# Layer 1 FFN: the down projection as seven products per half of the tokens, in program order

## The chip, the cores and the metric

The kernel runs on one core of one Trainium2 chip. The metric is the device time of one execution in microseconds (us). The core has five engines with queues of their own: PE (TensorE, matmuls), DVE (VectorE), ACT (ScalarE), POOL (GpSimd) and SP, which here issues DMAs. Only PE writes to PSUM by matmul; DVE and ACT read PSUM and SBUF; POOL works on SBUF.

## What is computed

Two layers over 2 x 1024 tokens of 512 dimensions, all in f32. Only the last part of layer 1 is touched:

```python
def _L1_ffn_ref(x, w_gate, w_up, w_down):
    h = jax.nn.silu(jnp.einsum('bsh,hi->bsi', x, w_gate)) * jnp.einsum('bsh,hi->bsi', x, w_up)
    h_sparse = _sparsify_2to4(h)   # of each four neighbours in i, the two largest by |h| stay
    return jnp.einsum('bsi,ih->bsh', h_sparse, w_down)

x = x + _L1_attn_ref(xn, ...) + _L1_ffn_ref(xn, ...)
```

`w_gate` and `w_up` are 512 x 2048, `w_down` is 2048 x 512.

## The kernel before

**Tiles.** The 2048 tokens are four blocks of 512, taken in two pairs (`pb`). The 2048 hidden dimensions are `G` = 4 groups of 512, so that there are eight groups of work in order (0 to 7: pair 0, then pair 1). A group has two units (`half` 0 and 1, "even" and "odd" units below; units 0 to 15), each of which computes 256 hidden dimensions for a pair of blocks. The order of the hidden dimensions is chosen so that the four members of a sparsity group lie in four chunks of the same partition: `h[:, c, :]`, c = 0..3.

**Gate and up.** `gate_up` computes a unit by Strassen's algorithm in the form of Winograd: seven products instead of eight. Each product is 4 matmuls of 128x128 weights and 512 columns. `combine_w` makes the four sums of weights (`s`) on POOL, `combine_x` the sums of tokens (`t_c`) on DVE. Three pairs of PSUM banks (`pa`, `pb`, `pc`) hold the products. On PE the order in a unit is: product 1 (`w1` x, to `pa`), 2 (`s[0]` `tt[0]`, to `pc`), 3 (`s[1]` `tt[1]`, to `pa`), 4 (`w1` x, to `pb`), 5 (`s[2]` `tt[2]`, to `pa`), 6 (`w2` `tt[3]`, to `pa`), 7 (`s[3]` y, to `pc`). ACT copies `pa` to SBUF after products 1 (L206), 3 (L214) and 5 (L219); DVE adds `pb` to the first copy (L201), `pc` to the third (L220) and to the second (L230). Silu is on ACT (L194), the multiplication by the up half on DVE (L197). After product n the helper calls `hook(n - 1)` (after the fourth, its add comes first): what `hook` issues stands there in the order.

**Sparsify.** Twelve steps over [128, 4, 512] of one block and group: one ACT operation (`ab`, absolute values, L1187) and eleven on DVE: `hi`, `lo` (L1188, L1189), two compares `first` (L1191, L1192), two into `both` (L1194, L1195), `way` (L1196), two adds to `first` (L1197, L1198), and two that set the smaller members of `h` to zero (L1201).

**Down.** `down` makes 128 tokens of one block: four matmuls of 512 columns (the chunks of a group) into one of two PSUM banks, then one DVE add to the residual `x1` (L1211), and in a pair's last group the store. Eight such calls belong to a group. `hook` issues up to four sparsify steps at a time and one or three downs at hooks 4 and 6 of a later unit.

**Order.** In this stage the framework's scheduler orders each engine's instructions; the layer 0 FFN and the attention use `in_program_order`, which chains the instructions of each of PE, DVE, ACT and POOL as the program issues them. The attention's last output projections (L828) all use the same PSUM bank, with a DVE add (L1017) after each; passes of unit 0 stand between them on PE.

**Transfers.** SP loads gate/up weights (`gu`, two tiles of 512 KB per unit, four buffers in the stage's own pool), down weights (`wd`, 1 MB per group, two buffers), and issues the stores, each as soon as what it waits for is done, in its queue's order.

Of the kernel before, what the change touches and what calls it, by code (L numbers as in the profile page):

```python
# [9 lines left out]
F32 = mybir.dt.float32  # L10
BF16 = mybir.dt.bfloat16
AF = mybir.ActivationFunctionType
ALU = mybir.AluOpType
PSUM = bass.MemoryType.PSUM

P = 128
B, S, D = 2, 1024, 512
N = B * S
TT = 512
# [4 lines left out]
G = 4  # L24
# [11 lines left out]
def two_layers(ctx: ExitStack, tc: tile.TileContext, t: dict, out: bass.AP):  # L36
# [8 lines left out]
    def mark():  # L45
        return len(nc.cur_bb.bb.instructions)
# [28 lines left out]
    def ps_bank(name, which):  # L75

        return ps.tile([P, 512], F32, tag=f"bank{which}", name=name)
# [68 lines left out]
    def combine_x(pool, x, y, name):  # L146

        tt = [
            pool.tile([P, 2, TT], F32, tag=f"t{n}", name=f"t{n}_{name}") for n in (1, 2, 4)
        ]  # L150
        tt.insert(2, y[:, :2, :])

        def first():
            nc.vector.tensor_sub(tt[0], y[:, :2, :], x[:, :2, :])  # L154
            nc.vector.tensor_sub(tt[1], y[:, 2:, :], tt[0])

        def second():
            nc.vector.tensor_sub(tt[2], y[:, 2:, :], y[:, :2, :])
            nc.vector.tensor_sub(tt[3], x[:, 2:, :], tt[1])

        return tt, first, second

    def combine_w(pool, w1, w2, name):
        s = [
            pool.tile([P, 2, 2, P], F32, tag=f"s{m}", name=f"s{m}_{name}") for m in range(1, 5)
        ]
        nc.gpsimd.tensor_add(s[0], w2[:, :, :2, :], w2[:, :, 2:, :])  # L167
        nc.gpsimd.tensor_sub(s[1], s[0], w1[:, :, :2, :])
        nc.gpsimd.tensor_sub(s[2], w1[:, :, :2, :], w2[:, :, :2, :])
        nc.gpsimd.tensor_sub(s[3], w1[:, :, 2:, :], s[1])  # L170
        return s
# [79 lines left out]
    with tc.tile_pool(name="a", bufs=1) as a:  # L251
# [355 lines left out]
        def down(n, i, half):  # L607


            h, js = h0[n, i], (2 * half, 2 * half + 1)  # L610
            up = i in hf_t and (i, half) not in joined
            if up:
                joined.add((i, half))
            banks = two_banks(f"acc_{n}_{i}_{half}")
            for bank, j in zip(banks, js):
                for m in range(2):
                    nc.tensor.matmul(  # L617
                        bank, h[:, m, j * P : (j + 1) * P], w2h[:, :, 2 * (n % NU) + m, :],
                        start=(m == 0), stop=(m == 1 and not up),
                    )  # L620
            if up:
                for bank, j in zip(banks, js):
                    rows = slice(32 * j, 32 * j + R + 1)
                    nc.tensor.matmul(
                        bank, hf_t[i][rows, j * P : (j + 1) * P], wup_aug[rows, :],
                        start=False, stop=True,
                    )
            for bank, j in zip(banks, js):
                r = x1[i][:, j, :]
                nc.vector.tensor_add(r, r, bank)  # L630
# [3 lines left out]
        def some_downs(n):  # L634
            for _ in range(min(n, len(downs))):
                down(*downs.pop(0))
# [514 lines left out]
                f(*args)  # L1151


    with tc.tile_pool(name="c", bufs=1, reuse_waits="tile") as c_:
        units = [(pb, g, half) for pb in range(2) for g in range(G) for half in range(2)]
        gu_w = dict(first_gu)

        def load_gu(n, m):

            pb, g, half = units[n]  # L1160
            w = gu_w[n, m] = c_.tile([P, 2, KC, P], F32, tag="w", name=f"gu_{n}_{m}", bufs=4)
            nc.sync.dma_start(out=w, in_=t["gu"][4 * g + 2 * half + m])

        wd = {}

        def load_down(n):

            g = n % G
            wd[n] = c_.tile([P, 4, D], F32, tag="wd", name=f"wd_{n}", bufs=2)
            nc.sync.dma_start(  # L1170
                out=wd[n],
                in_=t["down"][g * GW : (g + 1) * GW, :].rearrange("(p r) d -> p r d", r=4),
            )

        def sparsify(h, name):

            ab = c_.tile([P, 4, TT], F32, tag="ab", name=f"ab_{name}")
            pair = ab.rearrange("p (q two) n -> p q two n", two=2)
            hi = c_.tile([P, 2, TT], F32, tag="hi", name=f"hi_{name}")
            lo = c_.tile([P, 2, TT], F32, tag="lo", name=f"lo_{name}")  # L1180
            first = c_.tile([P, 4, TT], BF16, tag="first", name=f"first_{name}")
            win = first.rearrange("p (q two) n -> p q two n", two=2)
            both = c_.tile([P, 2, TT], BF16, tag="both", name=f"both_{name}")
            way = c_.tile([P, TT], BF16, tag="way", name=f"way_{name}")
            wide = way.unsqueeze(1).to_broadcast([P, 2, TT])
            v = nc.vector
            yield nc.scalar.activation(ab, h, AF.Abs)  # L1187
            yield v.tensor_tensor(hi, pair[:, :, 0], pair[:, :, 1], ALU.max)  # L1188
            yield v.tensor_tensor(lo, pair[:, :, 0], pair[:, :, 1], ALU.min)  # L1189

            yield v.tensor_tensor(win[:, :, 0], pair[:, :, 0], pair[:, :, 1], ALU.is_ge)  # L1191
            yield v.tensor_tensor(win[:, :, 1], pair[:, :, 0], pair[:, :, 1], ALU.is_lt)  # L1192

            yield v.tensor_tensor(both[:, 0], lo[:, 0], hi[:, 1], ALU.is_ge)  # L1194
            yield v.tensor_tensor(both[:, 1], lo[:, 1], hi[:, 0], ALU.is_gt)  # L1195
            yield v.tensor_sub(way, both[:, 0], both[:, 1])  # L1196
            yield v.tensor_add(first[:, 0:2], first[:, 0:2], wide)  # L1197
            yield v.tensor_sub(first[:, 2:4], first[:, 2:4], wide)  # L1198
            for q in range(2):
                c = slice(2 * q, 2 * q + 2)  # L1200
                yield v.scalar_tensor_tensor(h[:, c], first[:, c], 1.0, h[:, c], ALU.is_ge, ALU.mult)  # L1201

        def down(h, w, i, j, store):

            po = ps_bank(f"po_{w.name}_{i}_{j}", j % 2)
            for r in range(4):
                nc.tensor.matmul(  # L1207
                    po, h[:, r, j * P : (j + 1) * P], w[:, r, :], start=(r == 0), stop=(r == 3)
                )
            x = x1[i][:, j, :]  # L1210
            nc.vector.tensor_add(x, x, po)  # L1211
            if store:
                row = i * TT + j * P
                nc.sync.dma_start(out=out[row : row + P, :], in_=x)

        tt = None
        steps, downs = [], []

        def some_steps(n):

            while n and steps:
                if next(steps[0], None) is None:
                    steps.pop(0)
                else:
                    n -= 1

        def some_downs(n):
            for _ in range(min(n, len(downs))):
                down(*downs.pop(0))

        for n, (pb, g, half) in enumerate(units):
            i0, i1 = 2 * pb, 2 * pb + 1
            x, y = xt1[i0], xt1[i1]
            if g == half == 0:
                tt, *make = combine_x(c_, x, y, f"c{pb}")
                for f in make:
                    f()
            if n == 0:
                for m in range(2, 6):
                    load_gu(m // 2, m % 2)  # L1240
                load_down(0)
            if half == 0:
                h = [
                    c_.tile([P, 4, TT], F32, tag="h", name=f"h_{n}_{m}", bufs=4) for m in range(2)
                ]

            def hook(at):
                if at < 3 or half == 0 and at > 4:
                    some_steps(4)
                if at in (4, 6):  # L1250
                    some_downs(1 if at == 4 else 3)

            w1, w2 = gu_w.pop((n, 0)), gu_w.pop((n, 1))
            gate_up(
                c_, f"c{n}", w1, w2, combine_w(c_, w1, w2, f"c{n}"), x, y, tt,
                lambda m, i: h[i][:, 2 * half + m, :], hook,
            )
            if 1 <= n and n + 2 < len(units):
                load_gu(n + 2, 0)
                load_gu(n + 2, 1)  # L1260
            if half == 0 and n + 2 < len(units):
                load_down(n // 2 + 1)
            if half == 1:
                for m, i in enumerate((i0, i1)):
                    steps.append(sparsify(h[m], f"{n}_{m}"))
                    downs += [(h[m], wd[n // 2], i, j, g == G - 1) for j in range(NJ)]
        some_steps(12)
        some_downs(4)
        some_steps(12)
        some_downs(4)  # L1270


# [69 lines left out]
```

## Time and profile before

| | |
|---|---|
| median of 3 runs | 1920.13 us (1920.07 to 1932.04) |
| the profiled execution | 1923.83 us, its span 1922.1 us |
| mean granted TensorE clock | 0.987 |
| layer 1 FFN, first to last of its matmuls | about 1285 to 1918 us |
| DVE busy in an even and an odd unit (1404.0 to 1441.8, 1441.8 to 1479.5) | 24.5 and 14.6 us |
| POOL busy in the same two | 6.8 and 6.0 us |

The page gives, from one profiled execution, the busy time of each engine, its costliest groups of instructions (line, engine, tiles, shape, count, busy time, mean of one, and the idle time of the engine before them with what ended it), and the chain of work that ended last. A timeline row is: start in us, duration in us, engine, line, operation, tiles, shape, how many were merged, and in brackets the idle time before it and what ended it. A line number is one of the listing; where a helper issues the instruction, it is the helper's.

### The profile page before, as it was taken

To read this page: it belongs to the slowest core of one execution; us is meant where nothing else is said; L and a number is where in the kernel's file an instruction comes from. 1 tells how busy PE (TensorE), PEld (TensorE's weight loads), DVE (VectorE), ACT (ScalarE), POOL (GpSimd) and SP (SyncE) were. 2 spreads that over 40 slices of the span, in tenths; PEclk is the share of its full clock that TensorE was granted. 3 is DMA by queue.
4 is the path that set the end of the run, shared out by engine and by line. 5 is a ranking of instruction groups with operands and counts; after the bars stand their busy time and mean duration, and the time that the engine had idled before them with its cause. 6 is when DMAs were issued, how large, how long until landed. Compare 5 with 4: busy or idle time off the path is not lost.

```text
span 1922.1 us, 17085 instructions
## 1 busy us (share of the span) xinstructions
PE 1852.8 (96%) x6652; PEld 789.8 (41%) x6652; DVE 987.9 (51%) x1346; ACT 462.6 (24%) x646; POOL 610.8 (32%) x568
## 2 busy tenths in 40 slices
PE   6999999999999998999999989999999999999998
PEld 4444444444444443333333333334444444444443
DVE  3574353343443334755666656663753654735625
ACT  3221121111221111244333333331221211211210
POOL 3222232213432101366676647731111112111200
PEclk9899999999999999999999989999999999999999
DMA  6121111000100100000000000020111101211101
GB/s 231 39 77 33 33 33 33 22 22 33 43 29 23 43 5 23 1 12 12 1 12 12 24 11 12 12 77 0 44 44 33 55 26 62 77 33 44 44 1 44
DMA packets 29456, 68.00 MB, mean 35 GB/s; under 512 B 3392, under 2 KB 11584, under 8 KB 27840
## 3 DMA queue, kind: packets, MB, share of 16 engines
q1 hardware_dynamic: 28656, 66.61, 10.5%
q8 instruction: 53, 0.87, 0.2%
q10 hardware_dynamic: 720, 0.30, 0.1%
q14 instruction: 27, 0.22, 0.0%
HBM read 62.70 MB, written 4.19 MB: 35 GB/s over the span
## 4 chain that ended last, share of the span: by engine, by line
PE 87%; DVE 7%; issue 2%; ACT 2%; POOL 1%; DMA 1%; ACTq 0%; DVEq 0%; POOLq 0%
PE p_a L177 19%; PE p_c L177 18%; PE acc L617 12%; PE po_wd L1207 10%; PE pq L828 6%; PE m L880 4%; PE s L933 4%; PE o L975 3%; PE po L828 3%; PE pv L828 2%; DVE tops L888 1%; PE w L995 1%; POOL acc L983 1%; PE s L939 1%; DVE m L887 1%
## 5 line engine op out<-in xcount | busy, mean ns | idle before, releaser
L617 PE MATMUL acc<-w2h,h 128*128 128x512 f32 x512 | 230.1, 594 | 3.9 <-DVE y L529 1.8
L983 POOL TENSOR_TENSOR acc<-acc,pt 128x1024 f32<-128x1024 f32 (+3 forms) x138 | 233.7, 1715 | 0.0
L1207 PE MATMUL po_wd<-wd,h 128*128 128x512 f32 x512 | 226.5, 596 | 3.5 <-DVE h L1201 2.9
L888 DVE TENSOR_REDUCE tops<-m 128x2 f32<-128x1024 f32 (+2 forms) x192 | 180.8, 955 | 59.4 <-PE m L880 54.9
L630 DVE TENSOR_TENSOR x<-x,acc 128x512 f32<-128x512 f32 x128 | 86.2, 685 | 177.0 <-PE acc L617 140.3
L950 ACT ACTIVATE pt<-s 128x1024 f32<-128x1024 f32 (+3 forms) x160 | 115.0, 766 | 179.9 <-PE s L939 175.1
L1207 PEld LDWEIGHTS po_wd<-wd,h 128*128 128x128 f32 x512 | 97.7, 191 | 127.8 <-issue 119.0
L617 PEld LDWEIGHTS acc<-w2h,h 128*128 128x128 f32 x512 | 96.5, 190 | 124.1 <-issue 115.8
L828 PE MATMUL pq<-xt,wqk 128*128 128x512 f32 x256 | 128.1, 627 | 4.7 <-ACT qk L844 3.9
L887 DVE TENSOR_TENSOR m<-m,mask 128x256 f32<-128x256 f32 x128 | 54.7, 427 | 135.5 <-PE m L880 110.9
L177 PE MATMUL p_a<-t_a,s_a 128*128 128x512 f32 x256 | 119.6, 612 | 2.7 <-DVE t_a L154 2.7
L177 PE MATMUL p_a<-xt,w 128*128 128x512 f32 x256 | 119.7, 611 | 0.7 <-ACT xt L134 0.7
L177 PE MATMUL p_c<-xt,gu 128*128 128x512 f32 x256 | 116.2, 592 | 0.0
L177 PE MATMUL p_a<-xt,s_a 128*128 128x512 f32 x256 | 115.3, 593 | 0.0
L177 PE MATMUL p_c<-xt,s_c 128*128 128x512 f32 x256 | 115.1, 592 | 0.0
L177 PE MATMUL p_c<-t_c,s_c 128*128 128x512 f32 x256 | 112.5, 592 | 1.1 <-DVE t_c L154 1.1
L933 PE MATMUL s<-qk,qk 32*128 32x512 f32 (+3 forms) x768 | 99.8, 538 | 13.1 <-DVE tops L888 13.1
L880 PE MATMUL m<-qk,qk 32*128 32x512 f32 (+3 forms) x768 | 102.8, 536 | 5.9 <-ACT acc L950 3.0
L167 POOL TENSOR_TENSOR s_c<-gu 128x512 f32<-128x512 f32 x16 | 32.2, 2010 | 215.7 <-PE p_c L177 215.7
L177 PEld LDWEIGHTS p_a<-t_a,s_a 128*128 128x128 f32 x256 | 49.7, 197 | 66.5 <-issue 65.0
L177 PEld LDWEIGHTS p_a<-xt,w 128*128 128x128 f32 x256 | 49.1, 196 | 64.1 <-issue 63.1
L828 PEld LDWEIGHTS pq<-xt,wqk 128*128 128x128 f32 x256 | 44.8, 193 | 73.7 <-issue 61.2
(206 smaller groups left out, 2353.9 us busy)
## 6 DMA issues: line engine op xcount, KB each, us to landing
w<-in_W SPq DMA_DIRECT2D x32, 512.0 KB, 3.7
gu<-in_gu SPq DMA_DIRECT2D x32, 512.0 KB, 3.6
wd<-in_down SPq DMA_DIRECT2D x8, 1024.0 KB, 5.0
x<-in_x SPq DMA_DIRECT2D x16, 256.0 KB, 4.2
w2h<-in_W2q SPq DMA_DIRECT2D x4, 1024.0 KB, 11.8
xr<-in_x SPq DMA_DIRECT2D x16, 256.0 KB, 2.7
wqk<-in_WqkvT SPq DMA_DIRECT2D x16, 256.0 KB, 3.2
out_x<-x SPq DMA_DIRECT2D x16, 256.0 KB, 2.0
```

Source lines behind the costliest of these rows:

```text
L177: nc.tensor.matmul(pair[:, m, :], a[:, m, k, :], x[:, k, :], start=start and k == 0, stop=stop and k == 1, skip_group_check=True,)
L617: nc.tensor.matmul(bank, h[:, m, j * P : (j + 1) * P], w2h[:, :, 2 * (n % NU) + m, :], start=(m == 0), stop=(m == 1 and not up),)
L630: nc.vector.tensor_add(r, r, bank)
L828: nc.tensor.matmul(got[0], lhs(k), rhs(k), start=(k == 0), stop=(k == KC - 1))
L880: nc.tensor.matmul(pair[h // 2][:, h % 2, :e], q[rows, qt * P : (qt + 1) * P], k[rows, c * 512 : c * 512 + e], start=True, stop=True,)
L887: nc.vector.tensor_add(d, d, mask.unsqueeze(1).to_broadcast([P, 2, P]))
L888: nc.vector.tensor_reduce(out=tops[u][:, c, qt, 2 * p : 2 * p + 2], in_=pair[p][:, :, :e], axis=mybir.AxisListType.X, op=ALU.max,)
L933: nc.tensor.matmul(pair[h // 2][:, h % 2, s:], k[rows, kt * P : (kt + 1) * P], q[rows, cols], start=True, stop=False,)
L950: nc.scalar.activation(pt[:, :, s:], pair[p][:, :, s:], AF.Exp, scale=1.0 / math.sqrt(HD))
L975: nc.tensor.matmul(po[rows, s:], v[:, rows], pts[h // 2][:, h % 2, s:], start=(kt == 0), stop=last, tile_position=(0, h * HD),)
L983: eng.tensor_add(acc[:, :, s:], acc[:, :, s:], pt[:, :, s:])
L1207: nc.tensor.matmul(po, h[:, r, j * P : (j + 1) * P], w[:, r, :], start=(r == 0), stop=(r == 3))
```

## The change

The down projection of groups 0 to 6 becomes seven products as well. A half of the tokens of each block (`half`, 256 tokens of both blocks) is one problem: the 2 x 2 quarters of `h` are (block 0 or 1) x (chunks 0, 2 or 1, 3), the quarters of `wd` are (those chunks) x (halves of the 512 dimensions). `down_weights` makes four sums of weights per group on POOL (one in place), `down_hidden` four sums of hidden values per half on DVE (one in place). A product m (0 to 6) is four matmuls of 256 columns. Products alternate over the two banks: 0 and 2 accumulate in bank 0, 1 in bank 1, 3 and 5 in bank 1, 4 and 6 in bank 0. After product 0 ACT copies the bank; after product 1 DVE adds the copy and the bank to `u2`; after each of 2 to 6 DVE adds the bank to a quarter of the residual; POOL adds `u2` to three quarters (`add_u2`). Group 7 stays with plain matmuls (`row_down`).

`h` is one tile for both blocks, and sparsify goes by halves of tokens instead of by blocks. All is issued at places written out by hand: place p of group n is hook p mod 7 of unit 2n + 2 + p div 7. The second half's last products so fall into the next even unit (hooks 0, 1, 2 and 4), the first half's products 0 and 1 at hooks 5 and 6 of the even unit. What is left of group 6 stands behind unit 15, a sparsify step of group 7 between any two products, and then group 7. The stage is put in program order. `combine_w` of the next unit is issued at hook 5, `combine_x` of the second pair at unit 7's hook 5 and unit 8's start. Gate/up weights alternate between two buffers of the stage's pool and the two `wqk` buffers, and are loaded when the unit two before is done.

```diff
+    start2 = mark()
     with tc.tile_pool(name="c", bufs=1, reuse_waits="tile") as c_:
...
+        def load_gu(n):
+            pb, g, half = units[n]
+            for m in range(2):
+                pool, tag = (c_, "w") if n % 2 else (res, "wqk")
+                w = gu_w[n, m] = pool.tile([P, 2, KC, P], F32, tag=tag, name=f"gu_{n}_{m}", bufs=2)
+                nc.sync.dma_start(out=w, in_=t["gu"][4 * g + 2 * half + m])
...
+        def down_weights(n, last):
+            w11, w12, w21, w22 = quarters_w(n)
+            if not last:
...
+                nc.gpsimd.tensor_sub(td[n][0], w12, w11)
+                nc.gpsimd.tensor_sub(td[n][1], w22, td[n][0])
+                nc.gpsimd.tensor_sub(w12, w22, w12)
+            else:
+                nc.gpsimd.tensor_sub(td[n][2], w21, td[n][1])
+
+        def down_hidden(n, half):
...
+            nc.vector.tensor_sub(s3, h11, h21)
+            nc.vector.tensor_add(h21, h21, h22)
+            nc.vector.tensor_sub(s2, h21, h11)
+            nc.vector.tensor_sub(s4, h12, s2)
...
+        def down(n, half, m):
...
+            lhs, rhs = (
+                (h11, w11), (s2, t2), (h12, w21), (s1, t1), (s3, t3), (s4, w22), (h22, t4)
+            )[m]
...
+            for j in range(2):
+                for q in range(2):
+                    nc.tensor.matmul(
+                        out_[:, j, :], lhs[:, q, j * P : (j + 1) * P], rhs[:, q, :],
+                        start=m in (0, 1, 3, 4) and j == q == 0, stop=j == q == 1,
+                        skip_group_check=True,
+                    )
+            at = {2: (0, 0), 3: (1, 1), 4: (1, 1), 5: (0, 1), 6: (1, 0)}.get(m)
+            if m == 0:
...
+                nc.scalar.copy(held_d["e1"], out_)
+            elif m == 1:
...
+                nc.vector.tensor_add(held_d["u2"], held_d["e1"], out_)
+            else:
+                r = residual(n, half, *at)
+                nc.vector.tensor_add(r, r, out_)
+
+        def add_u2(n, half, *quarters):
+            for q in quarters:
+                r = residual(n, half, *q)
+                nc.gpsimd.tensor_add(r, r, held_d["u2"])
...
+        for n in range(groups - 1):
+            end = n == groups - 2
+            for half, steps in enumerate((
+                ((0, 1), (1, 4), (2, 4), (3, 3)), ((5, 1), (6, 3), (7, 3), (8, 3), (9, 2))
+            )):
+                for at, count in steps:
+                    put1(2 * n + 2, at, some_steps, n, half, count)
+            put1(2 * n + 2, 2, down_weights, n, False)
+            put1(2 * n + 2, 4, down_weights, n, True)
+            put1(2 * n + 2, 4, down_hidden, n, 0)
+            places = (
+                ((9, 11), ()) if end else ((5, 6, 7, 8, 9, 10, 11), (12, 13, 13, 14, 15, 16, 18))
+            )
...
+            if not end:
+                put1(2 * n + 2, 11, down_hidden, n, 1)
...
+                if at == 5 and n + 1 < len(units):
+                    unit_sums(n + 1)
+                if at == 5 and n % 2 == 0 and n:
+                    load_down(n // 2)
+                if at == 5 and n == len(units) // 2 - 1:
+                    next_tt, first, second = combine_x(c_, xt1[2], xt1[3], "c1")
+                    first()
...
+        for f, *args in tail:
+            f(*args)
+    in_program_order(start2)
```

## Prediction

> **What bounds the kernel now.** I read the page's busy table and its costliest groups first, then the chain that ended last over the layer 1 FFN (from 1400 us), then timelines of single engines.
>
> ```profile
> PE 1852.8 (96%) x6652; PEld 789.8 (41%) x6652; DVE 987.9 (51%) x1346; ACT 462.6 (24%) x646; POOL 610.8 (32%) x568
> ...
> L1207 PE MATMUL po_wd<-wd,h 128*128 128x512 f32 x512 | 226.5, 596 | 3.5 <-DVE h L1201 2.9
> ```
>
> PE is the busy engine, and the down projection had 3.5 us of idle in all. Every f32 matmul appears as two MATMUL records, which I call passes. The chain of one unit:
>
> ```profile
> 1449.87 3.43 PE po_wd L1207 x8
> 1453.30 6.87 PE p_c L177 x16
> 1460.17 10.30 PE po_wd L1207 x24
> 1470.47 17.17 PE p_c L177 x40
> ```
>
> The chain is PE without a gap; 24 passes in 10.30 us are 0.429 us each, and a unit (56 gate/up and 32 down passes) is 37.8 us. So PE work removed here is time removed, unless a wait replaces it.
>
> **PE work.** Before, 512 down passes: 512 x 0.429 = 219.8 us. After, groups 0 to 6 take 7 x 2 halves x 7 products x 4 matmuls x 2 = 784 passes of 256 columns; group 7 keeps 64 wide ones (27.5 us). The trace has no full-array f32 pass of 256 columns; the nearest rows are narrower (matmul and weight-load timelines in layer 0):
>
> ```profile
> 456.03 1.04 PE L131 MATMUL pt_d<-ident,z 128*128 128x128 f32 x8
> 456.91 2.31 PE L177 MATMUL p_a<-xt,s_a 128*128 128x512 f32 x5
> ...
> 362.24 1.87 PEld L476 LDWEIGHTS pp<-wp,xt 128*128 128x128 f32 x16
> ```
>
> Eight 128-column passes, each with its own weights, take 456.91 - 456.03 = 0.88 us: 0.110 each, so the load hides. A load alone repeats every 1.87/16 = 0.117. On the line from (128, 0.110) to (512, 0.429), 256 columns cost 0.216 us. Ends: half of 0.429, 0.215; and that plus an exposed load, 0.332. I take 0.216, since the 128-column row shows loads hidden behind an even shorter pass. After: 784 x 0.216 + 27.5 = 196.8. **Saved: 23.0 us**, 3.3 per group; a product of 8 narrow passes is 1.73 us.
>
> [...]
>
> **Start of the stage.** The instruction order on PE shows that before, 16 passes of unit 0 (its first and fourth products) stand in the gaps between the attention's output projections, each of which waits for DVE to empty the bank; after, only the first product's 8 do, since program order puts the fourth behind the second. The gaps stay: 8 x 0.429 = **+3.4**. The second product waits for DVE's t_c as before.
>
> **Units 0 to 2.** With no down product at hook 4, the sixth product (w2) waits for ACT's copy of the fifth. Before, the scheduler put passes of the next unit there. Layer 0 shows this wait once uncovered: 1.1 us idle before p_a<-t_a,w, released by ACT L219. Three units: **+3.3**. From unit 3 on a 1.73 us product covers it.
>
> **DVE and POOL in the even units.** Averages are harmless: DVE was busy 24.5 + 14.6 of two units' 75.5 us, and gains 4 adds and 8 down_hidden operations per group (12 x 0.60 start to start = 7.2). POOL gains ten operations of 1.26. But the two exclude each other, as these timelines show:
>
> ```profile
> 65.80 2.28 DVE L343 TENSOR_TENSOR w2xt<-w2xt 128x1024 f32<-128x1024 f32 x1
> 68.11 2.17 DVE L342 TENSOR_TENSOR w2h<-w2xt 128x1024 f32<-128x1024 f32 x1
> ...
> 64.75 2.25 POOL L376 TENSOR_TENSOR gamma_sb<-gamma_sb,dskip_tmp 128x512 f32<-128x512 f32 x1
> 66.96 2.24 POOL L377 TENSOR_TENSOR Wo_aug_sb<-Wo_aug_sb,Wo_by_tmp 128x512 f32<-128x512 f32 x1
> ...
> 1440.05 0.68 DVE L1194 TENSOR_TENSOR both<-lo,hi 128x512 bf16<-128x512 f32 x1
> 1441.37 1.37 DVE L1196 TENSOR_TENSOR way<-both 128x512 bf16<-128x512 bf16 x1
> ...
> 1439.65 2.81 POOL L167 TENSOR_TENSOR s_c<-gu 128x512 f32<-128x512 f32 x1 [14.99 <-PE p_c L177]
> ```
>
> At 64.75 they take turns: each DVE operation with both inputs in SBUF lasts 1.1 longer than its 1.22, each POOL operation 1.0 longer than its 1.26. At 1439.65 POOL let two DVE operations pass and got in where DVE waited for its own result; "way" (0.43 elsewhere) paid 0.95. DVE operations that read PSUM (L230, 1.22 beside POOL at 63.4) pay nothing.
>
> Now one even unit, in us from its start, PE ideal. Product 4 of the previous half ends at 2 x 3.43 + 2 x 1.73 = 10.3. Its residual add stands in DVE's order before the first sparsify operation, so sparsify starts at 11.1. At that moment POOL gets add_u2 and three of down_weights, four operations. Without POOL, DVE does hi, lo and two compares (4 x 1.14), product 5's add and four operations (2.8), and reaches the e1 add (L201) at 18.7, just before its input at 18.9; silu, then ACT's copy of product 5 of gate_up, end at 23.6, and the sixth product starts on time at 24.1. The residual add that frees the bank for the next half's product 0 ends at 25.9 (needed at 27.5). If all four POOL operations take turns with DVE (3.65, as the last is half beside an add from PSUM), L201 starts at 22.3, the copy ends at 25.1 and the sixth product is 1.1 late; down_weights' last operation, released at 24.3, costs 1.1 more, the bank is free at 29.8, and product 0 starts 2.4 late. If POOL waits for DVE's own gaps, DVE loses 2.3 and PE at most 0.2. I take 2.0: nearer to turns, since four operations must all fit before L201. Units 4, 6, ... 14: 6 x 2.0 = **+12.0**, ends 1.2 and 14.4. In unit 2 no earlier product holds DVE back; in odd units sparsify is spread over five hooks and DVE is free 5 us before L201.
>
> [...]
>
> **Tail.** Before:
>
> ```profile
> 1875.44 10.46 PE L1207 MATMUL po_wd<-wd,h 128*128 128x512 f32 x24
> 1888.85 29.43 PE L1207 MATMUL po_wd<-wd,h 128*128 128x512 f32 x64 [2.95 <-DVE h L1201]
> ```
>
> It loses 2.95 waiting, and the 64 passes take 29.3 instead of 27.5 (granted clock 0.93): 4.8. After, 96 narrow passes (12 products of group 6) cover the sparsify. Walking both queues from the end of unit 15, PE still waits for product 6's add (1.9, two sparsify operations stand between), for down_hidden of the second half (1.4), for the last add before group 7 (0.8) and for group 7's second half (2.0): 6.1. **+1.3**; ends -2 and +4.
>
> **At nothing.** Weight tiles in two pools and loads after a unit: landing in 3.6 to 5.0 us against 34 us until use. Output stores that SP now issues between weight loads hold back only loads with that lead. combine_w at hook 5 (5 us of POOL, 10 us before its use). combine_x split around unit 8. ACT's copies of product 0 (0.58, used 6.9 later). Without such cover each would cost its own duration.
>
> **Sum:** -23.0 + 3.4 + 3.3 + 12.0 + 1.3 = -3.0. The profiled execution took 1923.83 (span 1922.1): 1920.8. It lies 3.7 over the median of 1920.13; against that, **1917**.
>
> **Rivals.** *Contention hidden:* even units cost 0.2; -13.8, so 1906, or 1903 with a good tail. For it: 1439.65; against: 64.75. *DVE paces the down products (slower):* products alternate over two banks, so each waits for the add of the one two before; if turn-taking makes those adds late in odd units too, PE waits per product. 98 products at 0.2 us each give +20 on the forecast, 1937; from 0.23 each it is over 1% slower. Against: DVE's 5 us of slack there. *Narrow passes exposed (slower):* 0.332 instead of 0.216 is 784 x 0.116 = +91, 2008; every 10 ns cost 8 us. *The change does nothing to PE:* the order lists the 784 passes, so only the width can fail.
>
> **Chances.** Forecast (1910 to 1924) 0.52; contention hidden 0.21; DVE pacing 0.16; exposed passes 0.06; other 0.05. Under 1900.9 (1%, about what a measurement of this kernel can tell from no change) needs the hidden case and a perfect tail: 0.08. Over 1939.3: most of DVE pacing, exposed passes: 0.19. Within 1%: 0.73. Range 1903 to 1934.
>
> **What would show it.** Narrow passes: a product of 8 in 1.73 us in the chain. Start: 16 passes back to back of unit 0's third and fourth products where 8 filled gaps. Units 0 to 2: three idles of 1.1 on PE released by ACT L219. Even units: PE idle before p_c<-t_c,gu (ACT) and before product 0 (DVE's residual add), about 2 in all, and sparsify operations of 1.7 to 2.3 us. Tail: four waits on DVE, 6 in sum. I am wrong if PE's chain has no waits in units 4 to 14, if they stand before every down product, or if 8 narrow passes take much over 1.73.

## The result, and the profile after

No change that can be measured: 1923.34 us after (median of 20 runs, 1916.92 to 1936.26) against 1923.43 before (20 runs, 1917.77 to 1938.03), ratio 1.0003, 95% interval 0.9984 to 1.0022. The prediction was 1917, with 1903 to 1934 as its range and 0.73 on "within 1%".

The busy table of the profiled execution after (1916.92 us, span 1915.2; busy us, share of the span, instructions):

```profile
PE 1830.2 (96%) x6988; PEld 851.2 (44%) x6988; DVE 1079.6 (56%) x1430; ACT 468.2 (24%) x660; POOL 729.3 (38%) x638
```

PE is busy 22.6 us less than before. That this gain is missing in the medians, while the profiled span is 6.9 us shorter than before's, asks for care: two executions differ before the change even begins. In the attention, whose code is the same in both, a small DVE operation takes 5.38 us in the execution before:

```profile
1105.87 5.38 DVE L898 TENSOR_TENSOR tops<-tops 128x16 f32<-128x16 f32 x1
```

and in the one after, at the same step (both views are DVE timelines: start, duration):

```profile
1105.60 1.01 DVE L898 TENSOR_TENSOR tops<-tops 128x16 f32<-128x16 f32 x1
```

PE waits for it (5.53 us against 1.15), and by the last matmul with attention weights (L975), which ends at 1275.97 us before and 1268.53 after, the two executions are 7.4 us apart (4.4 of it here, most of the rest further on in the attention, at 1243 to 1249 us). So I compare from that matmul's end to the end of PE's last pass, which I call the FFN stretch: **642.3 us before, 642.8 after**. The stretch agrees with the medians; the spans do not, and no difference of a few us between two single spans says anything here.

The chain of waits after (start, duration, piece), from the fourth product of one even unit to its seventh, then the same place two units later, and then the tail:

```profile
1512.33 6.87 PE p_c L177 x16
1519.20 1.74 PE d L1287 x8
1520.94 0.02 issue
1520.96 0.63 ACT h L194
1521.59 0.91 ACT e_c L219
1522.50 0.04 issue
1522.55 3.71 PE p_c L177 x8
1526.26 0.36 issue
1526.62 1.96 PE d L1287 x8
1528.59 3.43 PE p_c L177 x8
...
1587.07 6.87 PE p_c L177 x16
...
1869.95 8.91 PE d L1287 x40
1881.43 14.02 PE dr L1341 x32
1896.16 1.15 DVE h L1250
1897.35 14.02 PE dr L1341 x32
```

Before, this stretch of the chain was PE alone. Now two units take 1587.07 - 1512.33 = 74.74 us, where 112 wide passes of 0.429 and 112 narrow ones of 0.2157 would be 72.2, and before 75.5. In each pair of units 3.3 us of work went and 2.5 of waiting came. The wait stands behind the product at hook 4: silu, ACT's copy, and only then the sixth product of gate/up.

Which wait ends last is named by the groups of 1280 to 1920 us (count | busy, mean | idle before, and what ended it):

```profile
L177 PE MATMUL p_c<-t_c,gu 128*128 128x512 f32 x128 | 58.5, 600 | 13.4 <-ACT e_c L219 13.4
L194 ACT ACTIVATE h<-e_c 128x512 f32<-128x512 f32 x48 | 30.2, 630 | 202.7 <-DVE e_c L230 66.1 <-PE d L1287 55.5 <-DVE e_c L201 48.8
```

PE waits for ACT's copy L219, as forecast. But of the silus in front of it, those that idle 55.5 us in all are released by PE's down product, not by DVE's L201. The timelines of ACT, DVE and POOL in an even unit show who is late:

```profile
1446.21 0.63 ACT L194 ACTIVATE h<-e_c 128x512 f32<-128x512 f32 x1 [9.25 <-PE d L1287]
1446.75 0.99 ACT L219 COPY e_c<-p_c 128x1024 f32<-128x1024 f32 x1
...
1433.07 1.22 DVE L1236 TENSOR_TENSOR hi<-ab 128x1024 f32<-128x1024 f32 x1
1434.20 2.29 DVE L1237 TENSOR_TENSOR lo<-ab 128x1024 f32<-128x1024 f32 x1
1444.29 1.22 DVE L201 TENSOR_TENSOR e_c<-e_c,p_c 128x1024 f32<-128x1024 f32 x1
...
1446.33 2.04 POOL L1207 TENSOR_TENSOR td<-wd,td 128x512 f32<-128x512 f32 x1 [4.28 <-PE d L1287]
```

L201 is late (its input was ready at 1441.0, since the fourth product is the first half of 16 passes from 1437.59), yet it is done at 1445.5 and silu starts at 1446.21, the moment the down product at hook 4 has ended (1446.18). Silu writes the tile `h` of a new group; `h` has two buffers, and the last reader of the older one is just that product: (h22, t4) of the second half of the group two before, put at place 18.

### The profile page after: what moved, and what is told of

Its sections match the earlier page's. It is cut to its first block, busy times and chain, and to the rows that moved or that the text cites. A ratio compares the mean times of both kernels' runs of the same rounds, so it can differ in the third digit from the quotient of the medians.

```text
span 1915.2 us, 17961 instructions
## 1 busy us (share of the span) xinstructions
PE 1830.2 (96%) x6988; PEld 851.2 (44%) x6988; DVE 1079.6 (56%) x1430; ACT 468.2 (24%) x660; POOL 729.3 (38%) x638
## 4 chain that ended last, share of the span: by engine, by line
PE 87%; DVE 5%; issue 3%; ACT 2%; POOL 1%; DMA 1%; SPq 0%; DVEq 0%; ACTq 0%; POOLq 0%
PE p_c L177 20%; PE p_a L177 19%; PE acc L617 12%; PE d L1287 8%; PE pq L828 6%; PE m L880 4%; PE s L933 4%; PE o L975 3%; PE po L828 3%; PE pv L828 2%; PE dr L1341 1%; DVE tops L888 1%; PE w L995 1%; POOL acc L983 1%; PE s L939 1%
## 5 line engine op out<-in xcount | busy, mean ns | idle before, releaser
L1306 POOL TENSOR_TENSOR x<-x,de 128x512 f32<-128x512 f32 x42 | 68.6, 1646 | 180.0 <-DVE x L1301 119.6
L1301 DVE TENSOR_TENSOR x<-x,d 128x512 f32<-128x512 f32 x70 | 47.8, 682 | 63.2 <-PE d L1287 63.2
L194 ACT ACTIVATE h<-e_c 128x512 f32<-128x512 f32 x48 | 30.2, 630 | 202.7 <-DVE e_c L230 66.1
```

The costliest lines, as they stand in the source:

```text
L1306: nc.gpsimd.tensor_add(r, r, held_d["u2"])
```

## The experiments

The theory after this reading, **A**: in the even units the wait is the buffer of `h`; DVE's lateness alone would leave about 1 us (an estimate: silu could have started at 1445.5 instead of 1446.21, so 0.7 of the 1.62 goes). The rival, **B**, is the prediction's: DVE and POOL take turns, so L201 and with it the copy are late. All runs but the last are single profiled executions; what is read from them is the waits and the FFN stretch.

**e1_swap.** The last two products of a second half change places, so that the one that reads `h` goes two hooks earlier.

```diff
-            yield down, n, half, 5
-            yield store, n, half, 0
-            yield down, n, half, 6
-            yield store, n, half, 1
+            last = ((5, 0), (6, 1)) if half == 0 or n == groups - 2 else ((6, 1), (5, 0))
+            for m, i in last:
+                yield down, n, half, m
+                yield store, n, half, i
```

> Only the order of the last two products of a group's second half is changed (the one that reads h goes to hook 2, the one that reads the sums sd to hook 4; groups 0 to 5). Theory A (the tile h has two buffers, so the first silu of a new group in an even unit waits for the last product that reads the h of two groups before, at hook 4): PE's wait before p_c<-t_c,gu in units 4, 6, ... 14 falls from 1.62 to about 1.0 us, which is what the late L201 alone would leave; the wait of 0.38 before the next half's first product goes too, because its bank is added out at hook 2; two units take 73.5 instead of 74.74 us, the FFN about 7 us less. Theory B (the prediction's: DVE and POOL taking turns make L201 and so the copy L219 late): the 1.62 stays, only the 0.38 goes, about 3 us less.

Neither came. The wait went up to 3.91 us, two units took 78.1, the FFN stretch 662.7. Silu is now released by DVE's L201, no longer by PE, so the buffer of `h` is free in time; but L201 is later. PE's, DVE's and POOL's timelines, and a row of the table of stretches (length, PE busy, PEld, DVE, ACT, POOL, PEclk, DMA share, GB/s):

```profile
1459.96 5.40 PE L177 MATMUL p_c<-t_c,gu 128*128 128x512 f32 x8 [3.91 <-ACT e_c L219]
...
1452.38 1.75 DVE L1243 TENSOR_TENSOR both<-lo,hi 128x512 bf16<-128x512 f32 x1
1454.17 1.38 DVE L1244 TENSOR_TENSOR way<-both 128x512 bf16<-128x512 bf16 x1
1455.58 1.63 DVE L1245 TENSOR_TENSOR first<-first,way 128x1024 bf16<-128x1024 bf16 x1
1457.13 1.21 DVE L201 TENSOR_TENSOR e_c<-e_c,p_c 128x1024 f32<-128x1024 f32 x1
...
1451.87 1.71 POOL L1207 TENSOR_TENSOR td<-wd,td 128x512 f32<-128x512 f32 x1
1453.55 1.71 POOL L167 TENSOR_TENSOR s_c<-gu 128x512 f32<-128x512 f32 x1
...
1460.00:1464.00 4.00, 4.00 (x6) 1.70 (x7) 4.00 (x6) 0.63 (x1) 0.00 (x0) 0.57 0.03 12
```

The product that was moved reads `td4` too. In the changed kernel POOL's last weight sum (L1207) had to wait for it, and with it everything behind it in POOL's queue. Released two hooks earlier, L1207 and the unit's gate/up sums ran beside DVE's short operations: `both`, `way` and the first add take 1.75, 1.38 and 1.63 where they took 0.68, 0.42 and 0.69. From `hi` to L201 it is 14.2 us instead of 11.2. A wait had shielded DVE from POOL. And a wait this long costs more than itself: the granted clock is 0.57 over the 4 us behind it (last row), which is 1.7 us lost; so it was behind five of the six.

**e2_early.** Sparsify's steps at hooks 0 to 3 are issued ahead of the down product of the hook; in the changed kernel the residual add of hook 1's product, which ends 4.6 us after `ab`, stood before `hi` in DVE's queue.

```diff
                 for at, count in steps:
                     put1(2 * n + 2, at, some_steps, n, half, count)
+                    if half == 0:
+                        here = between1[2 * n + 2, at]
+                        here.insert(0, here.pop())
```

> Only the place of sparsify's steps in the even units is changed: at hooks 0 to 3 they are issued before the down product of that hook instead of behind it, so DVE starts on them about 4.6 us earlier, right behind Abs, and L201 is no longer late. Theory A (h's buffer): the 1.62 us before p_c<-t_c,gu stay in units 4 to 14, because silu still waits for the product at hook 4; the 0.38 goes; about 3 us less. Theory B (DVE and POOL taking turns): both waits go, six units give 14 us back (two units 72.3 us).

It is as A expects. The chain of waits of this run, at an even unit:

```profile
1523.78 1.74 PE d L1287 x8
1525.52 0.02 issue
1525.54 0.63 ACT h L194
1526.17 0.91 ACT e_c L219
1527.08 0.04 issue
1527.12 3.70 PE p_c L177 x8
1530.82 1.88 PE d L1287 x8
```

L201 is on time now (it waits 1.39 us for its input from PE), and the 1.62 us in front of the sixth product stand as before to a hundredth, in all six even units; the 0.36 before the next down product is gone. The FFN stretch is 640.3, 2.5 less.

**e4_nosums.** The four sums of `down_weights` are left out for groups 1 to 6.

```diff
             w11, w12, w21, w22 = quarters_w(n)
-            if not last:
+            if n:
+                td[n] = td[0]
+            elif not last:
```

> Left out: the four weight sums of the down projection on POOL for groups 1 to 6 (the sums of group 0 are used for all, and w12 is not replaced). DVE's sparsify then meets only add_u2 and combine_w on POOL. Theory A (h's buffer): the 1.62 us before p_c<-t_c,gu stay in units 4 to 14, the 0.38 goes, about 3 us less. Theory B (turns between DVE and POOL): 1.62 goes as well, up to 14 us less.

It is as A expects again: 1.62 us in all six, FFN stretch 640.6. ACT's timeline names the releaser:

```profile
1455.56 0.63 ACT L194 ACTIVATE h<-e_c 128x512 f32<-128x512 f32 x1 [9.25 <-PE d L1289]
```

It isn't a clean removal, though: two of POOL's gate/up sums moved up into the gap, and `hi` to L201 still took 10.7 us. So this run says little about B; e2 is the clean test.

**e3_both.** The edits of e1_swap and e2_early together.

> The two edits of the swapped products and of the earlier sparsify together. Theory A: neither cause is left, no wait on PE from unit 3 to unit 13, two units take 72.2 us (112 wide passes at 0.429 and 112 narrow ones at 0.2157), the FFN 14 us less. Theory B expects the same here. If a wait stays, there is a third cause that neither names.

The chain of waits of this run, over the same two units as above:

```profile
1512.16 6.87 PE p_c L177 x16
1519.03 1.73 PE d L1287 x8
1520.76 3.43 PE p_c L177 x8
1524.19 1.73 PE d L1287 x8
...
1584.40 6.87 PE p_c L177 x16
```

No wait is left from unit 3 to the tail: two units take 72.24 us. The FFN stretch is 630.8, 12.0 less. The waits had cost 14.4 (worked out below); some 2.6 of that are taken back in this execution: the final 32 passes took 1.7 us longer after a wait of 1.92, and the attention's last projections 0.9. A row of the table of stretches (columns as above), with a clock of 0.62, stands for the first of the two; in the changed kernel's execution the same wait was followed by a clock of 1.00 (1897.3 to 1901.0):

```profile
1885.20:1889.00 3.80, 3.80 (x6) 1.69 (x7) 0.99 (x1) 0.00 (x0) 0.00 (x0) 0.62 0.09 31
```

**e9_nopool.** The swap, with all weight sums of POOL left out besides: those of the down projection for groups 1 to 6 and those of gate/up for units 4 to 15 (`s_of[n] = kept[3] if n > 3`, and e4's edit).

> The two products swapped as in the run of the swap alone (where PE's wait rose from 1.62 to 3.91 us, since the product that reads td4 left earlier and POOL's last down sum and three gate/up sums then met DVE's short operations before L201). Left out besides: the down projection's weight sums for groups 1 to 6 and the gate/up sums of units 4 to 15 (older sums are used), so POOL keeps only add_u2 there. Theory (two causes in a row: h's buffer and, behind it, DVE and POOL taking turns): with both gone no wait is left before p_c<-t_c,gu in units 4 to 14; from hi to L201 DVE takes about 8.5 us instead of 11.2 (changed kernel) and 14.2 (swap alone). Rival (DVE starts too late by itself, behind the residual add of hook 1): a wait of about 1 us stays.

No wait is left in units 4 to 14, and the FFN stretch is 630.8, as in e3. By DVE's timeline `hi` to L201 takes 8.6 us:

```profile
1443.22 1.22 DVE L1238 TENSOR_TENSOR hi<-ab 128x1024 f32<-128x1024 f32 x1
1451.82 1.22 DVE L201 TENSOR_TENSOR e_c<-e_c,p_c 128x1024 f32<-128x1024 f32 x1
```

So behind the buffer of `h` stands the turn-taking of B, and no third cause shows: with the buffer alone freed (e1) POOL decides, with DVE alone on time (e2) the buffer does.

**e6_wide.** Strassen's algorithm alone undone: eight 512-column passes for each 128 tokens of a block, in the same order and places.

```diff
-                ((9, 11), ()) if end else ((5, 6, 7, 8, 9, 10, 11), (12, 13, 13, 14, 15, 16, 18))
+                ((9, 11), ()) if end else ((5, 7, 9, 11), (12, 14, 16, 18))
...
+            for r in range(4):
+                nc.tensor.matmul(
+                    bank, hs[n][:, r, i, j * P : (j + 1) * P], wd[n][:, r, :],
+                    start=(r == 0), stop=(r == 3),
+                )
```

> Strassen's algorithm alone is taken out: groups 0 to 6 use four products of eight 512-column passes per half of the tokens, at places 5, 7, 9, 11 and 12, 14, 16, 18; program order, sparsify by halves and h's two buffers stay; no weight sums, hidden sums, u2. Theory (the saving on PE is real and is given back by waits): 448 wide passes of 0.429 take the place of 784 of 0.2157, +23.2 us; the 1.62 us before p_c<-t_c,gu stay, since silu still waits for the product at hook 4; the 0.38 goes (its bank is out earlier): about 20 us more than the changed kernel, two units 77.4 us. Rival (narrow passes cost more in place than 0.2157, or the sums on DVE and POOL take back what they save): under 10 us more.

Two units take 77.4 us, as expected, with the same 1.62. The FFN stretch is 658.2, 15.3 more than the changed kernel, not 20. From unit 2 to unit 14 it is 16.7 more, as the terms say. From there to the end 3.3 of work were added, and yet it is 1.1 less, because the idles in the tail are 2.1 in sum instead of 5.7. The expectation had left the tail out. The saving on PE is real.

**e7_sched.** The line `in_program_order(start2)` is left out.

> The line that fixes the instruction order of the layer 1 FFN is left out; the order is then chosen when the program is built. Theory (the waits at the start and in units 0 to 2 come from the fixed order, those of the even units from h's buffer): the start and units 0 to 2 give back 8 us, of the even units' 14 a part goes where another product is put in front of the one that waits: 8 to 16 us less. Rival (the fixed order is what keeps the narrow products' adds in step): new waits on DVE before the down products, 10 us more or worse.

The rival came, by far: the FFN stretch is 680.5, 37.7 more. The waits at the start and in units 0 to 2 shrank to 1.15 and 1.61, but the chain of waits has, in five even units,

```profile
1444.90 3.45 PE p_c L177 x8
1448.35 6.75 issue
1455.09 3.75 PE d L1287 x8
```

before the next half's first product. What stands there as "issue" ends as DVE's residual add ends (1454.31 + 0.68), which this order puts behind a row of sparsify steps. Some 16 of the 37.7 are slow passes behind these long waits (here 3.75 us for eight narrow ones instead of 1.73, and 4.58 for the next eight wide ones instead of 3.43). In the order chosen here the seven products take 38.2 us more in this stretch than the kernel before; what another order without the fixed one would give isn't shown.

**e5_ends.** The three places outside the even units: unit 0's fourth product is issued behind the first; the next unit's first product stands at hook 4 of units 0 to 2; in the tail two sparsify steps go ahead of the first wide product's add and `down_hidden` of group 6 into freed weight buffers, ahead of the tail.

```diff
+                if at == 4 and n < 3:
+                    begun[n + 1] = ps_pair(f"p0_c{n + 1}", turns % 3)
+                    products(
+                        begun[n + 1], gu_w[n + 1, 0][:, :, :2, :], x[:, :2, :], start=True
+                    )
...
+                (lambda: (y, tt)) if n == 0 else None, begun.get(n),
...
-        tail.append((some_steps, n, 1, 1))
+        tail.append((some_steps, n, 1, 3))
```

> Three edits at places that do not touch each other. Start: the fourth product of unit 0 (pb) is issued right behind the first, so 16 passes can stand in the attention's gaps as before the change: from the last of the attention's weighting matmuls to the end of unit 0, 3.4 us less. Units 0 to 2: the next unit's first product is issued at hook 4; the idles of 1.10, 1.10 and 1.44 before p_c<-t_c,gu go, and the 0.25 that PE's first passes take longer behind a wait: 4.4 us less. Tail: two sparsify steps of group 7's second half are moved ahead of the first wide product's add, which takes the last wait (1.92), and down_hidden of group 6's second half goes ahead of the tail into free weight buffers, which takes 1.2 to 2.5 of the other three: 3 to 5 us less. Sum 11 to 13. Rival: the waits are only moved (the bank pair that unit 0's fourth product takes, or the pair of the next unit's first product, comes free later than it is needed), and a new wait of 1 us or more shows behind each. The waits of the even units stay as they are in both.

Only a part came: the FFN stretch is 639.4, 3.4 less instead of 11 to 13. The 16 passes stand in the attention's gaps, the idles of units 0 and 1 are gone, and the tail's went from 5.7 to 3.1. But two waits are new, as the rival says, by PE's timeline:

```profile
1327.75 3.67 PE L177 MATMUL p_c<-xt,s_c 128*128 128x512 f32 x8 [1.15 <-issue]
...
1383.54 5.40 PE L177 MATMUL p_c<-xt,gu 128*128 128x512 f32 x8 [4.05 <-DVE e_c L201]
```

The fourth product, where it was, had covered ACT's copy L214; and in unit 2 the product that should cover takes the bank pair that L201 frees, and POOL's sums hold L201 back there: from `hi` to L201 it is 11.3 us, and 8.0 in e8_best, which makes group 0's sums earlier. Behind the 4.05 the eight passes took 5.40 us, 1.7 more than the 3.67 behind the 1.15.

**e8_best.** All edits of e3 and e5, with a repair for each new wait: half of unit 0's second product goes behind the third, and group 0's weight sums are made in unit 1.

```diff
-        products(pa, s[1], tt[1])
+        products(pa, s[1], tt[1]); len(cut) == 1 and products(pc, s[0], tt[0], start=True, blocks=(1,))
...
+            if n:
+                put1(2 * n + 2, 2, down_weights, n, False)
+                put1(2 * n + 2, 4, down_weights, n, True)
+            else:
+                put1(1, 3, down_weights, 0, False)
+                put1(1, 3, down_weights, 0, True)
```

> All edits together: swapped products, sparsify's steps ahead of the down products at hooks 0 to 3, and the three edits at the ends, with two repairs for what they ran into: in unit 0 the first half of the second product (s0) goes ahead of the third and its other half behind it, so that it covers ACT's copy again (the new wait of 1.15), and POOL's weight sums for group 0 are made in unit 1, so that unit 2's L201 is not late (the new wait of 4.05). Theory: from the last of the attention's weighting matmuls to PE's last pass the kernel before took 642.3 us and the one with the two even-unit edits 630.8, of which 1.7 at a low granted clock in the tail; 3.4 at the start, 4.4 in units 0 to 2 and 2.5 in the tail go as well: 618 to 620 us. As a whole about 1900 us against 1923, ratio 0.986 to 0.990. Rival (the waits of the ends are only moved again): 1 us in unit 0 and up to 4 in unit 2 come back, 623 us or more, ratio 0.990 to 0.993.

The FFN stretch is 618.7. Timed: 1903.29 us (6 runs, 1897.78 to 1905.37) against 1920.33 for the kernel before (11 runs), ratio **0.9895, 95% interval 0.9869 to 0.9921**: about 1% less, within what was expected. In its chain of waits one piece of 104 passes follows the wait for `t_c`, where the changed kernel waited twice more:

```profile
1318.42 44.89 PE p_c L177 x104
```

## Why the prediction was right, and where it was not

No change was forecast and came, and the time lies in the range. The sum was off by some 3 us: -3.0 forecast, -0.1 measured between the medians and +0.5 in the FFN stretch. The other 3.3 of the 6.3 between 1917 and 1923.34 are the reference: 1920.13 was the median of 3 runs, 1923.43 that of 20. Term by term, in us, waits priced with what PE really loses (see below):

| step | forecast | measured |
|---|---|---|
| PE work | -23.0 | -23.2: 784 x 0.2157 + 64 x 0.429, less 219.8 |
| start | +3.4 | +3.4: the same wait for `t_c`, 8 passes fewer done by then |
| units 0 to 2 | +3.3 | +3.6: 4.4 in waits of 1.10, 1.10, 1.44, less 0.8 for one wait before (0.57) that is gone |
| even units | +12.0 | +14.4: five of 2.5 and one of 1.9 |
| tail | +1.3 | +1.8: four waits of 1.70, 1.19, 0.86, 1.92, against 4.9 lost before |
| sum | -3.0 | 0.0 (0.5 in the stretch) |

**PE work** was right: a product of 8 narrow passes is 1.73 us in the chain, 0.2157 a pass, 0.503 of a wide one. The load stays hidden: exposed, it would have made a pass 0.332 by the forecast's estimate. **Start** and **tail** went as forecast, the tail's waits within 0.25 each.

**Units 0 to 2** had the three idles. That unit 2 would add nothing, since "no earlier product holds DVE back", was wrong by 0.34: POOL's sums lie beside sparsify there too, and without the down sums (e6) it is 1.20 instead of 1.44.

**The even units** were right in size and wrong in the step that gave it. The turn-taking is as forecast: `lo` and both compares take 2.29 (the compares 1.21 in e9, where POOL makes no weight sums), POOL's operations 2.1 to 2.3, and L201 starts 3.3 us after its input (forecast 3.4). But the step from there to "the sixth product is 1.1 late" isn't what happened: the sixth product was 1.62 late because silu waited for the last reader of the old `h`, a wait that the forecast does not have. e2 removes DVE's lateness and the 1.62 stays; e3 and e9 show that both must go. The second wait, in front of product 0, has the forecast's cause: it ends as DVE's residual add does (1451.10 + 0.67). But "product 0 starts 2.4 late" in all came to 1.62 + 0.38 = 2.00 of idle. That 2.0 was also the chosen value is chance: a cause that the forecast missed made up for one that was smaller than forecast. (The forecast's own figures give 29.8 - 27.5 = 2.3 where it has 2.4, and 11.1 + 4.56 + 2.8 = 18.5 where it has 18.7; neither bears on the choice.)

**The size** was missed by what an idle figure leaves out. A pass is recorded as 592 ns and the next starts 429 ns after it, so idle counted from a pass's end begins 0.16 late, and the first interval after a wait is 0.11 longer. Each wait costs PE 0.24 to 0.27 more than its figure. In the even units that is 2.8 us for 11 waits. Less the 0.38 of a second wait, which unit 14 does not have, it is the 2.4 between 12.0 and 14.4.

Of the rivals, contention hidden did not come, nor did DVE pacing every product (no waits in odd units), nor exposed narrow passes.

Two things stay open. A third buffer for `h` alone (16 KB more in each partition) wasn't tried. And e3 was executed once, so its 12 us stand on single executions.

## What to carry to other kernels

When a wait has been traced to one engine, look for a second one that ends a little earlier, buffers' last readers included; two causes in a row hide each other, and removing only one left the wait as it was (e2, 1.62 us) or made it longer (e1, 3.91). Before a dependency is loosened, list what is queued behind the instruction that it holds, on its engine: it will run at the freed moment, beside what is there (in e1 `way` went from 0.42 to 1.38 us). A product that fills a gap should be priced by what its old place covered as well (1.15 us in e5).

## What the runs showed of the hardware

Behind long waits PE's passes were slow as well: the eight wide passes behind the 3.91 us in e1 took 5.40 us, at a granted clock of 0.57 over 4 us; behind the 1.62 of the changed kernel eight took 3.70. In the layer 1 FFN of the eleven traces PE had 73 waits of 0.9 to 1.7 us, and none was followed by slow passes; of 15 waits of 1.9 or 2.0 us, four cost 1.1 to 1.8 us more at a reduced clock, with the same wait in the same place sometimes free and sometimes not; of 14 from 2.9 to 6.8 us, 13 cost 1.6 to 3.0 more.

One DVE operation on 128x16 elements in the attention (L898), which comes eight times in an execution and takes about 1.0 us in most of them, took 4.8 to 5.4 once in seven of the eleven traces, at different places of the stage; in the execution before PE waited for it. With the 4.4 us that it cost there, and some 1.7 for each wait that is followed by slow passes, single executions move by more than the 3.0 forecast for this change. What causes it is open.
